# Carrying keys between chunks on VectorE, transposing the query norms, and replacing the hand-placed pieces of a one-core transformer kernel

## The chip, the cores and the metric

The kernel runs on one core of a Trainium2 chip. A core has five engines that each take their instructions in order: TensorE (PE; its weight loads are listed apart as PEld), VectorE (DVE), ScalarE (ACT), GpSimd (POOL) and SyncE (SP), which here only issues DMAs. The metric is the device time of one execution in microseconds (us), less is better.

## The reference

Everything is float32. Tokens are 2048, features 128. A block of six local-attention layers with feed-forward is applied to x, its result is added by half, a linear-attention block follows, and the six layers are applied again, also by half. Cut to what the change touches, one layer is:

```
xa  = token_shift(layer_input)                 # half of the features come one token later
q, k, v = split(xa @ Wqkv)                     # 16 heads of 64
q, k = l2norm(q) * q_scale, l2norm(k) * k_scale
q = q*cos*scale + rotate_half(q)*sin*scale     # scale grows with the token's number
k = k*cos/scale + rotate_half(k)*sin/scale
# windows of 32 queries look at their own 32 keys and the 32 before
sim  = 8 * q_window @ k_two_windows.T ; mask ; softmax ; @ v_two_windows ; @ Wo
x = xa + attention ; x = x + feed_forward(layer_norm(x))
```

A rotation by position depends only on the difference between query and key. The kernel therefore counts positions afresh in every chunk of 256 tokens, so that one table serves all chunks; the last 32 keys of a chunk, which the next chunk's first window needs, must then be turned by 256 positions into the next chunk's frame. That turn is a 2x2 mixing of the two halves of a head's features: with constants c and s per frequency, new1 = c*old1 - s*old2 and new2 = c*old2 + s*old1.

## The kernel before

**Tiling.** Activations lie transposed, features on partitions and tokens along the free axis. A layer is cut in `NAC` = 8 chunks of `AC` = 256 tokens; a chunk's attention has `STEPS` = 4 steps (two halves of 128 tokens by two groups of 8 heads). The feed-forward (`feed_forward`, L590 on) works on 512 tokens at a time, so it recurs every second chunk. There are 12 layer passes with the linear block after six.

**Order.** No scheduler decides: each function is cut in pieces by `yield`, and the table `POS` (L33 to L83) gives each piece a place (step relative to its chunk, position within the step). The pieces of all chunks are sorted by that place and emitted, which fixes each engine's queue. So in steady state the pieces of several chunks are interleaved in a pattern that repeats every four steps, and every eight steps with the feed-forward.

**One chunk, in the order of its data.**
- `project`: four groups of products (L288) give q and k in PSUM, in two feature halves. `rotate` multiplies them with the tables on VectorE (L297, "prod") and adds the two products on GpSimd (L303) into the tiles `abq` and `abk`. ScalarE squares the raw values (L309, "sq"), GpSimd adds the halves of the squares (L323), and `square_sums` sums them over features by a product on TensorE (L331, "ss").
- `norms` (L402 to L410) makes the inverse norms `rn` from `ss`: a row per head, tokens along the row. For the queries `query_norms` brings them to one row per token: two products with a selection matrix `sel[:, 2]` (L418, tile "nt"), then a copy (L424, "rq"). For the keys `spread_norms` sends them through DRAM and back as `rk`.
- `scale_keys` (called at `sk0` and `sk1` for the two groups of heads) multiplies `abk` by `rk` on VectorE (L447) and then calls `gather`, which copies keys by DMA from `abk` into `hk`, columns 32 on (L395).
- `earlier_keys` fills columns 0 to 31 of `hk`: a product of the previous chunk's last keys with the constant matrix `rot_m` (L459, tile "pk") and a ScalarE copy (L460); for a layer's first chunk a memset.
- `similarities` (L475 mask, L485 products, L497 and L498 maxima), `exponentials` (L510, with the per-row scale from `rq`), `normalised` (L520 reciprocal on VectorE, L522 multiply on GpSimd), `transposed` (L535 on TensorE, L541 copy), `values` (L562, copies L569 and L571), `output` (L578, L587).

GpSimd's queue in a step is: L522 for an earlier step, the two L323 additions, then the two L303 additions. On TensorE, L331 for a group pair stands right after L288 of the next step and ahead of L347.

Of the kernel before, what the change touches and what calls it, by code (L numbers as in the profile page):

```python
# [8 lines left out]
F32 = mybir.dt.float32  # L9
BF16 = mybir.dt.bfloat16  # L10
AF = mybir.ActivationFunctionType
ALU = mybir.AluOpType
# [3 lines left out]
P = 128  # L16
# [17 lines left out]
    "tabq": [(-11, 129), (-10, 188)],  # L34
    "tabk": [(-9, 19), (-9, 166)],
    "ss": [(-6, 25)],
    "vwin": [(0, 76)],
    "gq0": [(-6, 100)],
    "gq1": [(-4, 78)],
    "e0": [(0, 95)],  # L40
    "e1": [(0, 96)],
    "nrm": [(1, 108)],
    "qn": [(-3, 127)],
    "ek": [(-1, 91)],
    "proj": [(-9, 150), (-8, 42), (-8, 44), (-8, 45), (-8, 48), (-8, 156)],
    "vproj": [(-2, 26), (-2, 90)],
    "norms": [(-4, 47), (-4, 82), (-4, 125)],
    "rk": [(-4, 206), (-3, 27)],
    "sk0": [(-2, 94)],
    "sk1": [(-1, 176)],  # L50
    "te": [(2, 62), (2, 64)],
    "av": [(2, 149), (2, 189), (2, 190)],
    "out": [(4, 112), (4, 134)],
    "sim": [(0, 73), (0, 74), (0, 75)],
    "ff": [(11, 101), (12, 34), (12, 106), (13, 7), (13, 170), (14, 131), (15, 124), (15, 143),
        (16, 17), (16, 42), (16, 143), (16, 159), (17, 51), (17, 140), (17, 192), (18, 50),
        (18, 58), (18, 148), (18, 162), (21, 146), (21, 199)],
    "ff2": [(12, 128), (12, 194), (13, 179), (14, 65), (14, 99), (15, 52), (15, 118), (15, 147),
        (16, 20), (16, 23), (16, 122), (16, 123), (16, 130), (16, 151), (16, 152), (16, 153),
        (16, 203), (17, 5), (17, 40), (17, 97), (17, 169)],  # L60
    "ff3": [(10, 182), (10, 184), (10, 186), (10, 194), (10, 198), (10, 200), (10, 204), (11, 2),
        (11, 4), (11, 13), (11, 24), (11, 35), (11, 36), (11, 37), (11, 120), (11, 133),
        (11, 139), (11, 157), (11, 181), (11, 183), (11, 193)],
    "start0": [(-19, 114), (-17, 104), (-16, 84), (-16, 168), (-13, 41), (-10, 79)],
    "start1": [(-11, 126), (-9, 70), (-7, 31), (-7, 142), (-7, 158), (-6, 141)],
    "start2": [(-9, 19), (-7, 29), (-5, 136), (-5, 205), (-4, 11), (-4, 121)],
    "start3": [(-4, 12), (-4, 16), (-4, 46), (-4, 88), (-3, 6), (-2, 28)],
    "sums0": [(-9, 1), (-9, 49), (-8, 43), (-8, 165), (-8, 174), (-7, 43), (-7, 137), (-6, 30)],
    "sums1": [(-1, 92), (-1, 119), (0, 72), (0, 77), (1, 38), (1, 39), (2, 161), (2, 184)],
    "sums2": [(1, 185), (1, 201), (2, 167), (2, 202), (3, 63), (3, 93), (3, 160), (4, 113)],  # L70
    "sums3": [(3, 195), (4, 15), (4, 80), (4, 81), (4, 144), (4, 145), (4, 177), (4, 191)],
    "kv": [(5, 3)],
    "outs0": [(5, 9), (5, 14), (5, 109), (5, 111), (5, 173), (5, 175), (6, 54), (6, 68), (6, 71),
        (6, 138), (7, 55), (7, 61), (7, 69), (7, 135)],
    "outs1": [(6, 60), (11, 83), (11, 110), (12, 18), (13, 53), (13, 67), (13, 180), (14, 98),
        (14, 163), (15, 32), (15, 56), (15, 102), (15, 154), (17, 87)],
    "outs2": [(6, 10), (13, 21), (13, 89), (13, 164), (14, 171), (14, 178), (14, 196), (15, 33),
        (15, 116), (15, 143), (16, 66), (16, 85), (16, 132), (17, 22)],
    "outs3": [(5, 172), (15, 115), (15, 155), (16, 117), (17, 86), (17, 105), (18, 8), (18, 103),
        (18, 107), (18, 162), (18, 197), (19, 57), (19, 59), (19, 187)],  # L80
# [14 lines left out]
def kernel(ctx: ExitStack, tc: tile.TileContext, a: dict, out: bass.AP):  # L95
# [9 lines left out]
    def small(name):  # L105
        return ps_small.tile([P, CH], F32, tag="small", name=name)
# [49 lines left out]
    sq_consts = keep([P, 3, P], "sq_consts", src=a["squares"].rearrange("p a b -> p (a b)"))  # L156
    ident, hmask, rot_m = (sq_consts[:, i, :] for i in range(3))
    wqk = [load_qk(0, g) for g in range(4)]
    qks = keep([P, DEPTH, 2, 2], "qks", src=a["qks"])
    sel = keep([P, 3, 32], "sel", src=a["sel"].rearrange("p a b -> p (a b)"))  # L160
# [112 lines left out]
    def project(l, c, g):  # L273
# [3 lines left out]
        if g % 2 == 0:  # L277
            for qk, bufs in (("q", 2), ("k", 4)):
                d[qk, g // 2] = work.tile(
                    [P, 2, 2, AC], F32, tag=f"ab{qk}", name=f"ab{qk}_{nm}", bufs=bufs  # L280
                )
# [13 lines left out]
        def rotate(s):  # L295
            prod = work.tile([P, 2, 2, AC], F32, tag="prod", name=f"prod{s}_{nm}", bufs=2)
            nc.vector.tensor_tensor(  # L297
                prod,
                both[s].unsqueeze(2).to_broadcast([P, 2, 2, AC]),
                tabs[l, s].rearrange("p (u v) t -> p u v t", u=2),  # L300
                ALU.mult,
            )
            nc.gpsimd.tensor_tensor(  # L303
                d["qk"[s], g // 2][:, :, g % 2, :], prod[:, 0], prod[:, 1], ALU.add
            )
# [70 lines left out]
    def gather(l, c, qk, g2):  # L376


        d = chunk(l, c)
        off = 0 if qk == "q" else WIN  # L380
        if g2 == 0:
            d["h" + qk] = work.tile(
                [P, 8, off + AC], F32, tag=f"h{qk}", name=f"h{qk}_{d['nm']}"
            )
        for j in range(2):
            src = d[qk, g2][64 * j : 64 * j + 64]
            first = 4 * g2 + 2 * j
            if qk == "q":
                nc.sync.dma_start(
                    d["hq"][:, first : first + 2, :].rearrange("p i t -> p (i t)"),  # L390
                    src.rearrange("p u i t -> p u (i t)"),
                )
            else:
                for i in range(2):
                    nc.sync.dma_start(d["hk"][:, first + i, WIN:], src[:, :, i, :])  # L395
# [17 lines left out]
    def query_norms(l, c):  # L413

        d = chunk(l, c)
        nt = small(f"nt_{d['nm']}")
        for t in range(2):
            nc.tensor.matmul(  # L418
                nt[:, HEADS * t : HEADS * t + HEADS],
                d["rn"][:, t * P : (t + 1) * P], sel[:, 2, 0:HEADS],  # L420
                start=True, stop=True,
            )
        rq = work.tile([P, 2, HEADS], F32, tag="rq", name=f"rq_{d['nm']}", bufs=2)
        nc.vector.tensor_copy(rq.rearrange("p t h -> p (t h)"), nt[:, 0 : 2 * HEADS])  # L424
        d["rq"] = rq

# [16 lines left out]
    def scale_keys(l, c, g2):  # L443
        d = chunk(l, c)
        k = d["k", g2].rearrange("p u i t -> p u (i t)")
        r = d["rk"][:, 2 * g2 : 2 * g2 + 2, :].rearrange("p i t -> p (i t)")
        nc.vector.tensor_tensor(k, k, r.unsqueeze(1).to_broadcast([P, 2, CH]), ALU.mult)  # L447
        gather(l, c, "k", g2)

    def earlier_keys(l, c):  # L450

        d = chunk(l, c)
        first = d["hk"][:, :, 0:WIN]
        if c == 0:
            nc.gpsimd.memset(first, 0.0)
            return
        ps = small(f"pk_{d['nm']}")
        ps3 = ps[:, 0 : 8 * WIN].rearrange("p (h t) -> p h t", h=8)
        nc.tensor.matmul(ps3, rot_m, chunks[l, c - 1]["hk"][:, :, AC:], start=True, stop=True)  # L459
        nc.scalar.copy(first, ps3)  # L460

    def similarities(l, c, step):
# [31 lines left out]
        rq = d["rq"][:, t, 8 * h8 : 8 * h8 + 8].rearrange("p (i r) -> p i r", r=2)  # L494
        for par in range(2):
            yield
            nc.vector.tensor_reduce(peaks[par], sims[par], AX.X, ALU.max, negate=True)  # L497
            nc.vector.tensor_tensor(st8[:, 0, :, par], peaks[par], rq[:, :, par], ALU.mult)  # L498

    def exponentials(l, c, step, par):  # L500
# [7 lines left out]
        rq = d["rq"][:, t, 8 * h8 : 8 * h8 + 8].rearrange("p (i r) -> p i r", r=2)  # L508
        for i in range(4):
# [3 lines left out]
                scale=rq[:, i, par : par + 1],  # L513
# [75 lines left out]
    def feed_forward(layer, f):  # L589
# [52 lines left out]
        if final:  # L642
            x = work.tile([P, CH], F32, tag="gate", name=f"last_{nm}", bufs=1)
# [33 lines left out]
    def linear_sums(f):  # L677
# [14 lines left out]
        lo = work.tile([P, CH], F32, tag="gate", name=f"lo_{f}", bufs=1)  # L692
# [40 lines left out]
    def linear_out(f):  # L733
# [11 lines left out]
        z = work.tile([P, CH], F32, tag="gate", name=f"lz_{f}", bufs=1)  # L745
# [47 lines left out]
    for l in range(2 * DEPTH):  # L793
# [12 lines left out]
        for c in range(NAC):  # L806
# [15 lines left out]
            put("ek", t0, earlier_keys, l, c)  # L822
# [27 lines left out]
def _shape_constants():  # L850
# [20 lines left out]
    c, s = np.diag(back * np.cos(AC * inv)), np.diag(back * np.sin(AC * inv))  # L871
    one = np.block([[c, -s], [s, c]]).reshape(2, 32, 2, 32).transpose(1, 0, 3, 2).reshape(64, 64)
    rot_m = np.kron(np.eye(2), one)
# [11 lines left out]
        [r[:, None] == r[None, :], r[:, None] // 8 == r[None, :] // 8, rot_m], 1  # L885
    ).astype(np.float32)

    sel = np.zeros((P, 3, 32), np.float32)
    for i in range(2):
        sel[r, i, 4 * i + r // 32] = 2.0**18  # L890
    for h in range(HEADS):
        sel[32 * (h // 2 % 2) + 4 * (h // 8) + 2 * (h // 4 % 2) + h % 2, 2, h] = 1.0
    return {
        "rot": rot,
        "band": band,
# [61 lines left out]
```

## Time and profile before

| what | value |
|---|---|
| median of 3 runs | 3454.14 us (3449.54 to 3456.67) |
| the profiled execution | 3449.61 us |
| its span in the trace | 3447.8 us, so 1.8 us lie around it |
| mean granted TensorE clock | 0.982 |
| TensorE busy | 96% of the span |
| VectorE, ScalarE, GpSimd busy | 77%, 72%, 63% |
| busy share of the 16 DMA engines, queue q1 | 53.7% |

A profile row of a group names line, engine, operation, written tile <- read tiles and shapes, then the count, the busy time and the mean of one. A timeline row gives the start in us from the span's start, the length, the engine and the same names; in square brackets stands the idle time before it with what ended it. Matmul records overlap, since TensorE pipelines: what a group costs is read from its start to the next group's start. A float32 matmul shows as two records, a transpose as one. The slices of the page show that TensorE is nearly full except at the start, between the two halves of the kernel (1.6 to 1.9 ms, the linear block) and at the end.

### The profile page before, as it was taken

Reading aid. Unit: us, or ns where it says so; the run is one execution under the profiler, and the core shown is the slowest. Engines: PE = TensorE matmul, PEld = TensorE weight load, DVE = VectorE, ACT = ScalarE, POOL = GpSimd, SP = SyncE. Lnnn points to the kernel's source line nnn. Section 1 sums busy time; section 2 is a strip of 40 time slices with the busy share of each in tenths; the row PEclk is TensorE's granted clock in tenths of the full one; section 3 lists DMA queues with packets and bytes.
Section 4 is the critical chain, followed back from the end, with each engine's and each line's share of the span. In section 5 each row is a group of like instructions: output and inputs, shape, how many; then the busy total and the mean of one; then the engine's idle time right before and its main releaser. Section 6 shows DMA issues by size and latency. Waiting matters only on the chain. (4 is left out here: it accounts for less than half of the span.)

```text
span 3447.8 us, 153348 instructions
## 1 busy us (share of the span) xinstructions
PE 3293.9 (96%) x64088; PEld 2280.2 (66%) x64088; DVE 2658.6 (77%) x5068; ACT 2491.0 (72%) x8613; POOL 2182.2 (63%) x2195
## 2 busy tenths in 40 slices
PE   6999999999999999999678999999999999999998
PEld 3776776676667676676334766766767766766665
DVE  5787888878778788786446887887878888787785
ACT  4777777777777777776446777777777777777775
POOL 6766666667667667663136766666666666666661
PEclk8999999999999999999889999999999999999999
DMA  4665565556556556554004665566565565565552
GB/s 134 145 150 135 141 152 142 136 150 147 133 146 153 132 143 156 139 135 121 28 13 100 144 150 142 135 153 147 133 153 143 135 153 142 139 150 138 144 134 73
DMA packets 356445, 459.91 MB, mean 133 GB/s; under 512 B 52396, under 2 KB 218664, under 8 KB 355752
## 3 DMA queue, kind: packets, MB, share of 16 engines
q1 hardware_dynamic: 355752, 450.11, 53.7%
q8 instruction: 504, 8.26, 1.0%
q14 instruction: 189, 1.55, 0.1%
HBM read 96.53 MB, written 2.62 MB: 29 GB/s over the span
## 5 line engine op out<-in xcount | busy, mean ns | idle before, releaser
L510 ACT ACTIVATE e<-sim,st,rq 128x64 f32<-128x64 f32 x3072 | 1196.0, 410 | 352.6 <-DVE st L498 322.8
L297 DVE TENSOR_TENSOR prod<-p,tab 128x1024 f32<-128x1024 f32 x768 | 936.1, 1222 | 293.4 <-ACT sq L309 202.1
L288 PE MATMUL p<-xa,wqk 128*128 128x256 f32 x3072 | 776.5, 395 | 13.6 <-DVE xa L242 4.8
L303 POOL TENSOR_TENSOR abq<-prod 128x512 f32<-128x512 f32 x384 | 490.7, 1278 | 398.3 <-DVE prod L297 364.3
L522 POOL TENSOR_TENSOR e<-e,st 128x512 f32<-128x512 f32 x384 | 451.8, 1177 | 425.5 <-DVE st L520 242.8
L309 ACT ACTIVATE sq<-p 128x512 f32<-128x512 f32 x768 | 438.8, 603 | 350.5 <-PE ss L331 159.2
L303 POOL TENSOR_TENSOR abk<-prod 128x512 f32<-128x512 f32 x384 | 492.4, 1282 | 242.6 <-DVE prod L297 217.8
L510 ACT ACTIVATION_READ_ACCUMULATOR e<-sim,st,rq 128x1 f32 x3072 | 643.3, 209 | 0.0
L288 PEld LDWEIGHTS p<-xa,wqk 128*128 128x128 f32 x3072 | 557.7, 191 | 105.8 <-issue 9.8
L323 POOL TENSOR_TENSOR sq<-sq 128x256 f32<-128x256 f32 x768 | 580.1, 776 | 0.2
L562 PEld LDWEIGHTS av<-eT,vw 64*64 64x64 f32 x18432 | 392.3, 135 | 227.8 <-ACT hk L460 59.6
L562 PE MATMUL av<-eT,vw 64*64 64x32 f32 x18432 | 434.9, 221 | 2.9 <-DVE eT L541 1.8
L347 PE MATMUL pv<-wv,xa 128*128 128x512 f32 x768 | 417.5, 626 | 7.8 <-DVE oT L571 7.8
L578 PE MATMUL y<-oT,wo 128*128 128x128 f32 x3072 | 390.5, 280 | 0.2 <-DVE oT L571 0.2
L578 PEld LDWEIGHTS y<-oT,wo 128*128 128x128 f32 x3072 | 362.5, 192 | 36.1 <-issue 22.6
L562 PE MATMUL av<-eT,v 64*64 64x32 f32 x6144 | 384.3, 219 | 0.0
L535 PEld LDWEIGHTS te<-sq_consts,e 128*128 128x128 f32 x1536 | 188.5, 141 | 236.1 <-issue 166.9
L497 DVE TENSOR_REDUCE sim<-sim 128x4 f32<-128x256 f32 x768 | 325.9, 424 | 21.6 <-PE sim L485 20.7
L485 PE MATMUL sim<-hk,hq 64*32 64x64 f32 x24576 | 333.3, 223 | 0.1
L562 PEld LDWEIGHTS av<-eT,v 64*64 64x64 f32 x6144 | 318.8, 135 | 0.0
L612 PE MATMUL pf<-xc,w 128*128 128x512 f32 (+1 forms) x576 | 304.6, 615 | 11.5 <-POOL xc L600 9.3
L485 PEld LDWEIGHTS sim<-hk,hq 64*32 64x32 f32 x24576 | 306.0, 105 | 0.3
(140 smaller groups left out, 4270.9 us busy)
## 6 DMA issues: line engine op xcount, KB each, us to landing
hq<-abq SPq DMA_DIRECT2D x384, 256.0 KB
hk<-abk SPq DMA_DIRECT2D x768, 128.0 KB
vw<-v SPq DMA_DIRECT2D x768, 128.0 KB
rk<-rkd SPq DMA_DIRECT2D x384, 128.0 KB
vw<-v SPq DMA_DIRECT2D x744, 64.0 KB
wqk<-in_Wqk SPq DMA_DIRECT2D x48, 256.0 KB
tab<-in_rot SPq DMA_DIRECT2D x24, 512.0 KB
wv<-in_Wv SPq DMA_DIRECT2D x24, 256.0 KB
```

The costliest lines, as they stand in the source:

```text
L288: nc.tensor.matmul(both[s][:, u, :], wqk[g][:, 2 * s + u, :], xs, start=True, stop=True)
L297: nc.vector.tensor_tensor(prod, both[s].unsqueeze(2).to_broadcast([P, 2, 2, AC]), tabs[l, s].rearrange("p (u v) t -> p u v t", u=2), ALU.mult,
L303: nc.gpsimd.tensor_tensor(d["qk"[s], g // 2][:, :, g % 2, :], prod[:, 0], prod[:, 1], ALU.add)
L309: nc.scalar.activation(sq, both[s], AF.Square)
L323: nc.gpsimd.tensor_tensor(sq[:, 0, :], sq[:, 0, :], sq[:, 1, :], ALU.add)
L347: nc.tensor.matmul(ps, xa[:, ti * P : (ti + 1) * P], wv[j], start=True, stop=True)
L485: nc.tensor.matmul(sims[par][WIN * b : WIN * b + WIN, i, :], d["hq"][rows, 4 * h8 + i, at : at + WIN], d["hk"][rows, 4 * h8 + i, at : at + ...
L497: nc.vector.tensor_reduce(peaks[par], sims[par], AX.X, ALU.max, negate=True)
L510: nc.scalar.activation(e[:, i, par, :], d["sims", step][par][:, i, :], AF.Exp, bias=st8[:, 0, i, par : par + 1], scale=rq[:, i, par : par ...
L522: nc.gpsimd.tensor_tensor(ef, ef, st8[:, 1].rearrange("p i r -> p (i r)").unsqueeze(2).to_broadcast([P, 8, SK]), ALU.mult,)
L562: nc.tensor.matmul(av[u][r : r + 64, m, WIN * b : WIN * b + WIN], d["vs", t][u][b][:, at : at + DH], d["eT", step][64 * u : 64 * u + 64, i ...
L578: nc.tensor.matmul(y[:, 0:P], wo[:, i, :], d["oT", t].rearrange("p h u m q -> p (h u m) q")[:, i, :], start=(i == 0), stop=(i == 7),)
```

## The change

1. **Keys of the chunk before.** `abk` gets 32 more columns per head group in front. After scaling a chunk's keys, VectorE writes the turned last 32 keys into the front of the *next* chunk's `abk`, with per-partition constants `turn` (c, s, -s): one tensor_scalar over 128 columns and two scalar_tensor_tensor over 64 columns. `gather` then copies 288 columns instead of 256, and `earlier_keys` with its product, its PSUM tile and its ScalarE copy is gone. In a layer's last chunk there is no turn; in its first the memset moves to `abk`, once for each group.
2. **Query norms.** The two products with `sel[:, 2]` become two transposes of `rn` by `ident`; the copy picks 32 of the transposed columns; `step_norms` gives the later readers their heads in the new order.
3. **Memory.** `rot_m` and `sel[:, 2]` go, `turn` (128x3) comes. The tile `gate` (512 columns) goes, and its users at the ends of the two halves and in the linear block take a half of a `prod` tile.
4. **Places.** `POS` is new throughout. Compared by the built instruction order, TensorE, ScalarE and VectorE keep their order within the repeating pattern, apart from what items 1 and 2 remove and add: VectorE has the three turn instructions directly behind each L447. SP issues one weight load earlier by one or two places in three spots of a layer. In the linear block the fourth tile's pieces (`outs3`) come later than before, behind the first tile's, and a few pieces near the kernel's start change places.

```diff
     def scale_keys(l, c, g2):
         d = chunk(l, c)
-        k = d["k", g2].rearrange("p u i t -> p u (i t)")
-        r = d["rk"][:, 2 * g2 : 2 * g2 + 2, :].rearrange("p i t -> p (i t)")
-        nc.vector.tensor_tensor(k, k, r.unsqueeze(1).to_broadcast([P, 2, CH]), ALU.mult)
+        k = d["k", g2]
+        r = d["rk"][:, 2 * g2 : 2 * g2 + 2, :].unsqueeze(1).to_broadcast([P, 2, 2, AC])
+        nc.vector.tensor_tensor(k[..., WIN:], k[..., WIN:], r, ALU.mult)
+        if c == 0:
+            nc.gpsimd.memset(k[..., 0:WIN], 0.0)
         gather(l, c, "k", g2)
-
-    def earlier_keys(l, c):
-
-        d = chunk(l, c)
-        first = d["hk"][:, :, 0:WIN]
-        if c == 0:
-            nc.gpsimd.memset(first, 0.0)
-            return
-        ps = small(f"pk_{d['nm']}")
-        ps3 = ps[:, 0 : 8 * WIN].rearrange("p (h t) -> p h t", h=8)
-        nc.tensor.matmul(ps3, rot_m, chunks[l, c - 1]["hk"][:, :, AC:], start=True, stop=True)
-        nc.scalar.copy(first, ps3)
+        if c + 1 < NAC:
+
+            last, first = k[..., AC:], chunk(l, c + 1)["k", g2][..., 0:WIN]
+            nc.vector.tensor_scalar(first, last, turn[:, 0:1], None, ALU.mult)
+            for u in range(2):
+                nc.vector.scalar_tensor_tensor(
+                    first[:, u], last[:, 1 - u], turn[:, u + 1 : u + 2], first[:, u],
+                    ALU.mult, ALU.add,
+                )
```

```diff
     def query_norms(l, c):
-        nt = small(f"nt_{d['nm']}")
+        nt = small(f"nt_{d['nm']}").rearrange("p (t r) -> p t r", t=4)
         for t in range(2):
-            nc.tensor.matmul(
-                nt[:, HEADS * t : HEADS * t + HEADS],
-                d["rn"][:, t * P : (t + 1) * P], sel[:, 2, 0:HEADS],
-                start=True, stop=True,
-            )
-        rq = work.tile([P, 2, HEADS], F32, tag="rq", name=f"rq_{d['nm']}", bufs=2)
-        nc.vector.tensor_copy(rq.rearrange("p t h -> p (t h)"), nt[:, 0 : 2 * HEADS])
+            nc.tensor.transpose(nt[:, t, :], d["rn"][:, t * P : (t + 1) * P], ident)
+        rq = work.tile([P, 2, 2, 8], F32, tag="rq", name=f"rq_{d['nm']}", bufs=2)
+        nc.vector.tensor_copy(rq, nt[:, 0:2, 0:64].rearrange("p t (i r) -> p t i r", r=32)[..., 0:8])
         d["rq"] = rq
+
+    def step_norms(d, t, h8):
+
+        return d["rq"][:, t, :, 4 * h8 : 4 * h8 + 4].rearrange("p i (j r) -> p j i r", r=2)
...
-            put("ek", t0, earlier_keys, l, c)
```

## The prediction

> **What bounds the kernel now.** First the page: TensorE's busy share and its row of slices, then VectorE's row.
>
> ```profile
> PE 3293.9 (96%) x64088; PEld 2280.2 (66%) x64088; DVE 2658.6 (77%) x5068; ACT 2491.0 (72%) x8613; POOL 2182.2 (63%) x2195
> ...
> PE   6999999999999999999678999999999999999998
> ...
> DVE  5787888878778788786446887887878888787785
> ```
>
> TensorE is full outside the start, the middle and the end, so at first sight whatever leaves its queue is won. But a busy share can hold waits, so next comes the timeline of TensorE over one four-step pattern (columns: start, length, group).
>
> ```profile
> 1009.09 0.60 PE L535 MATMUL te<-sq_consts,e 128*128 128x128 f32 x4
> 1009.62 0.30 PE L475 MATMUL sim<-band,ident_b 64*32 64x256 bf16 x8
> ...
> 1010.51 0.70 PE L459 MATMUL pk<-hk,sq_consts 128*128 128x256 f32 x2
> 1011.05 1.02 PE L210 MATMUL mean<-xf,mean_w 128*128 128x512 f32 x2
> ...
> 1014.99 1.20 PE L331 MATMUL ss<-sq,sel 128*32 128x256 f32 x8
> 1016.12 1.13 PE L347 MATMUL pv<-wv,xa 128*128 128x512 f32 x2
> ...
> 1026.52 0.62 PE L418 MATMUL nt<-sel,rn 128*128 128x16 f32 x4
> 1026.99 2.82 PE L637 MATMUL yf<-h,w 128*128 128x512 f32 x6
> ```
>
> Start to start, "pk" costs 0.54 us, "nt" 0.47, four transposes 0.53 (0.13 each). And "ss" takes 1.13 here; at 1032.73 the same eight records take 0.57. So 0.56 us is a wait inside a queue that looks full. It recurs in every second chunk (1082.31, 1148.11 and 1213.92 also take 1.13). The wait view names the squares that GpSimd adds (L323). What are these late for? VectorE and GpSimd in the same stretch:
>
> ```profile
> 1001.57 1.22 DVE L297 TENSOR_TENSOR prod<-p,tab 128x1024 f32<-128x1024 f32 x1 [2.94 <-ACT sq L309]
> ...
> 1005.16 1.22 DVE L447 TENSOR_TENSOR abk<-abk,rk 128x1024 f32<-128x1024 f32 x1
> 1006.30 0.19 DVE L520 RECIPROCAL st<-st 128x8 f32<-128x8 f32 x1
> ...
> 1011.94 0.19 DVE L520 RECIPROCAL st<-st 128x8 f32<-128x8 f32 x1
> 1012.05 1.18 DVE L447 TENSOR_TENSOR abk<-abk,rk 128x1024 f32<-128x1024 f32 x1
> ```
>
> ```profile
> 1012.28 1.85 POOL L522 TENSOR_TENSOR e<-e,st 128x512 f32<-128x512 f32 x1 [0.48 <-DVE st L520]
> 1014.09 1.41 POOL L323 TENSOR_TENSOR sq<-sq 128x256 f32<-128x256 f32 x2
> ```
>
> From 1001.57 VectorE has no gap until 1015.5. Its second reciprocal (1011.94) releases GpSimd's L522, L323 follows in GpSimd's queue and ends at 1015.50, and "ss" ends 0.6 later. Backward, the product at 1001.57 waited for ScalarE's square, and ScalarE is busy without a gap from 991.35, where it waited for TensorE's L288. So from 991 to 1015.5 a chain ScalarE, VectorE, GpSimd runs *beside* TensorE and ends 0.56 later than it. Both "nt" (993.60) and "pk" of this chunk lie beside that chain.
>
> The other kind of chunk (even numbers, with L618 ahead of the second L447) is near the same edge:
>
> ```profile
> 1177.73 1.04 POOL L522 TENSOR_TENSOR e<-e,st 128x512 f32<-128x512 f32 x1 [0.21 <-DVE st L520]
> 1178.74 2.39 POOL L323 TENSOR_TENSOR sq<-sq 128x256 f32<-128x256 f32 x2
> ```
>
> L323 ends at 1181.13, "ss" starts at 1181.30: 0.17 us of slack. Of four such chunks in a layer two are like this, one waits 0.4 (1115.06) and one 1.3 (1048.17).
>
> **Part 1, products removed.** TensorE loses 84 "pk" of 0.54 us: 45 us. "nt" becomes two transposes, by the row of "te" 2 x 0.13 = 0.27 for 0.47: 0.20 x 96 = 19 us. Were TensorE the bound everywhere: 3449.6 - 64 = 3386. ScalarE loses 84 copies of 0.37; its exponentials there wait for VectorE's L498 anyway, so nothing.
>
> **Part 2, the turn.** Each of 168 L447 gets three VectorE instructions behind it. No row has just these. The nearest for the tensor_scalar has its very size, SBUF to SBUF:
>
> ```profile
> L730 DVE TENSOR_SCALAR wl_kv<-sq_consts,wl_ksum x1: 286/286/286, 1719.6 to 1719.6; 128x128 f32<-128x128 f32 x1
> ```
>
> [...] For 64 columns of scalar_tensor_tensor: L662 takes 425 ns at 256, L727 292 at 128, so 225 at 64; L409 (371 at 256) gives 170. I take 0.20. A dependent instruction starts 0.04 after its forerunner (1010.87 + 0.42 to 1011.33), an independent one 0.08 before its end (1006.30). The next instruction moves by 0.04 + 0.29 + 0.04 + 0.20 + 0.12 = **0.69 us** (bounds 0.5 and 0.8). That is 116 us more of VectorE, to some 80% of the span, and it isn't spread: at the first L447 of a chunk it stands ahead of the L520 that releases GpSimd, in a stretch without a gap.
>
> *Odd chunks* (1, 3, 5; 7 has no turn): L323 ends at least 0.69 later; TensorE comes 0.74 earlier and waits the more. Absolutely +0.69.
> *Even chunks* (0, 2, 4, 6): GpSimd's own queue from L522 (1171.63) to 1177.52 carries part; L522 moves by 0.5 to 0.7, less 0.17 slack.
>
> [...] L447 reads two tensors in SBUF. Its row of before:
>
> ```profile
> L447 DVE TENSOR_TENSOR abk<-abk,rk x192: 1172/1225/4678, 56.6 to 3383.1; 128x1024 f32<-128x1024 f32 x192
> ```
>
> At 1012.28 L522, 1.04 us elsewhere, takes 1.85 while L447 runs; at 1045.04 an L447 takes 4.63 and ends 1.08 after a GpSimd run that lasted to 1048.6. [...] I take 0.2 for L323, and keep 0 and the long wait for the range.
>
> **Edits costed at nothing, with their cover.** The extra wait of the turn on the copy that last read its target is for a copy one chunk (35 us) old. The key copies are issued behind L447, not behind the turn, and are an eighth larger on queues at 54%. The weight loads that SP issues earlier (0.4 to 0.7 us each) delay `rk`, issued by 1031.5 and needed at 1037.0. The extra memsets are 12 of some 0.2 us (estimate from L455's 0.3) on GpSimd. Half a `prod` tile for `gate`: a rotation may wait for it at two layer ends and in the linear block, 0 to 4 us in all. In the linear block the fourth tile's step leaves the place ahead of the first tile's layer norm; its four VectorE instructions of 0.7 us were in the way there, 3 us gained, and 6 lost or gained are the bounds.
>
> **Sum.** Odd chunks with a turn: 0.69 + 0.2 = 0.9, three in a layer: 2.7. Even chunks: two with slack 0.7 each (0.69 + 0.2 - 0.17), one without 0.9, and the one at 1048.17 1.4, since there TensorE also waited (1050.06) for VectorE's L571 *behind* the second L447, so both turns count: 3.7. The gain of "nt" in four even chunks lies outside the chain: -0.8. Per layer 5.6, twelve layers 67. At the two starts of the layers no feed-forward fills VectorE for some eight chunks; the removed products are gained there instead: -6. Linear block: -3. 3449.6 + 58 = **3508 us**, against a median of 3454 in the runs shown (the profiled execution is 4.5 below it): 1.6 to 1.7% slower.
>
> **Rivals.**
> 1. *TensorE is the bound after all: faster.* For it: 96% busy, and "ss" waits in half the chunks only. Against: the steady 0.56 us, and the 0.17 of slack. It needs the 0.69 us to vanish on VectorE: slack of 0.7 in front of L520. VectorE's idle before 1001.57 (2.9 us) isn't such slack, since it ends with ScalarE's square. With half to all of the 64 us: 3386 to 3420. It decides if the turn delays L323 by less than about 0.1 us per chunk.
> 2. [...] If each second turn waits for GpSimd's run to end, VectorE is 1.4 to 2 us later; its 0.75 us of idle at 1016.27 takes part, and some 0.8 us reach TensorE in 84 chunks: 67 us more, 3575. For it: ten L447 of over 4.5 us. [...]
> [...]
> 4. *It doesn't do what it says:* the instruction order shows the products gone and three instructions behind each L447; no chance given.
>
> **How the numbers follow.** The forecast 0.65 (its own range 3478 to 3540), rival 1 0.18, rival 2 0.09, rival 3 0.08. The range leaves out the lower part of rival 1 and most of rival 2: 3412 to 3550. No change is within 0.2% (7 us), about what a measurement of this kernel can tell. Faster takes rival 1 and a little of rival 3: 0.19; no change 0.05; slower 0.76.
>
> **What would show it.** Right: "ss" (L331) at some 2 us instead of 1.13 in odd chunks and 1.5 to 2 instead of 0.57 in even ones, with L323 named; TensorE's busy share down to 93 or 94%; the three turn instructions together near 0.7 us at the first L447 of a chunk and longer at the second; L522 or L323 lengthened there. Wrong: "ss" still at 0.57 to 1.2, or the turn in a gap of VectorE. If the span falls by 45 to 64 us, the chain wasn't the bound, and step "VectorE has no gap ahead of L520" failed. If L323 moved as said but TensorE gained elsewhere, the sum over chunks failed, not its step.

## The result, and the profile after

| | median of runs, us | profiled execution: span, us | granted clock |
|---|---|---|---|
| before | 3454.22 (3449.54 to 3456.67, 4 runs) | 3447.8 | 0.982 |
| after | 3511.96 (3505.87 to 3515.56, 4 runs) | 3513.7 | 0.981 |

The ratio is 1.0167, with a 95% interval of 1.0148 to 1.0186: 1.7% slower. The profiled execution of after is the longest of its runs (3515.56 us) and that of before one of the shortest, so the spans differ by 65.9 us and the medians by 58. First the page of after: engines (busy us, share of the span, instructions) and two rows of slices.

```profile
PE 3275.3 (93%) x63728; PEld 2222.5 (63%) x63728; DVE 2849.6 (81%) x5572; ACT 2468.5 (70%) x8529; POOL 2181.4 (62%) x2207
...
PE   6999999999999999998778999999999999999998
...
DVE  6888888888888888886537888888888888888885
```

TensorE has 360 matmuls less and is busy for 93% instead of 96%. VectorE got 191 us more, to 81%, and now shows an 8 in nearly every slice: most of its slices of 7 are filled. GpSimd's sum is as it was (2182.2 before). Next TensorE's waits, of after and of before (what waited, for what, us, times, longest):

```profile
PE ss L332 <- POOL sq L324: 71.3, 99, 4.8
PE p L289 <- ACT v L352: 33.8, 42, 1.4
...
PE p L289 <- DVE xf L588: 10.2, 32, 0.4
```

```profile
PE ss L331 <- POOL sq L323: 25.7, 15, 3.5
PE te L535 <- ACT oT L569: 20.0, 33, 1.1
```

The wait at "ss" has grown as forecast. Two waits were next to nothing before (4.2 and 0.2 us): "p" for ScalarE's copy of v, and "p" for VectorE's L588. The wait of "te" for ScalarE is gone from the list. (Lines of after: L446 is the key scaling, L453 and L455 the turn, L521 the reciprocal, L523 GpSimd's product, L324 its squares, L332 "ss", L588 the addition of the output.)

Now the turn itself, in the timeline of VectorE of after, at the first key scaling of an odd chunk and at its second:

```profile
1027.22 1.23 DVE L446 TENSOR_TENSOR abk<-abk,rk 128x1024 f32<-128x1024 f32 x1
1028.48 0.29 DVE L453 TENSOR_SCALAR abk<-abk,turn 128x128 f32<-128x128 f32 x1
1028.81 0.48 DVE L455 SCALAR_TENSOR_TENSOR abk<-abk,turn,abk 128x64 f32<-128x64 f32 x2
1029.20 0.20 DVE L521 RECIPROCAL st<-st 128x8 f32<-128x8 f32 x1
1029.32 0.54 DVE L588 TENSOR_TENSOR xf<-y,xa 64x128 f32<-64x128 f32 x2
...
1034.92 1.17 DVE L446 TENSOR_TENSOR abk<-abk,rk 128x1024 f32<-128x1024 f32 x1
1036.13 0.95 DVE L453 TENSOR_SCALAR abk<-abk,turn 128x128 f32<-128x128 f32 x1
1037.11 1.32 DVE L455 SCALAR_TENSOR_TENSOR abk<-abk,turn,abk 128x64 f32<-128x64 f32 x2
```

From the start of L446 to that of the reciprocal it is 1.98 us, against 1.14 before (1005.16 to 1006.30): the first turn costs 0.84. The second lasts from 1036.13 to 1038.43, 2.3 us, and GpSimd is at work beside it (over all second turns of after it is 1.5 us in most even chunks, 2.3 in most odd ones, 1.9 on average):

```profile
1035.15 1.85 POOL L523 TENSOR_TENSOR e<-e,st 128x512 f32<-128x512 f32 x1 [0.47 <-DVE st L521]
1036.96 1.40 POOL L324 TENSOR_TENSOR sq<-sq 128x256 f32<-128x256 f32 x2
```

These two GpSimd rows are as long as before (1.85 and 1.41). What reaches TensorE, in the same chunk (the last column names the wait):

```profile
1028.52 1.13 PE L289 MATMUL p<-xa,wqk 128*128 128x256 f32 x4
1030.00 1.10 PE L289 MATMUL p<-xa,wqk 128*128 128x256 f32 x4 [0.35 <-DVE xf L588]
1030.94 1.02 PE L348 MATMUL pv<-wv,xa 128*128 128x512 f32 x2
...
1037.26 0.62 PE L332 MATMUL ss<-sq,sel 128*32 128x256 f32 x2
1038.41 0.63 PE L332 MATMUL ss<-sq,sel 128*32 128x256 f32 x6 [0.53 <-POOL sq L324]
1038.97 1.13 PE L348 MATMUL pv<-wv,xa 128*128 128x512 f32 x2
```

The same "p" and "pv" before:

```profile
1006.40 1.99 PE L288 MATMUL p<-xa,wqk 128*128 128x256 f32 x8
1008.23 1.02 PE L347 MATMUL pv<-wv,xa 128*128 128x512 f32 x2
```

Eight "p" and the step to "pv" took 1.83 us; here 2.42. "ss" takes 1.71 instead of 1.13, start to start. A third wait of an odd chunk stands two steps later: "nt" starts 0.31 later, since it waits for ScalarE's squares. Together 0.59 + 0.58 + 0.31, less the 0.54 of "pk", which is gone, come to 0.94 us, which is what such a chunk loses.

One stretch of an odd chunk will be used below: from the "p" of the step ahead of "ss" (1028.52) to the "pv" behind "ss" (1038.97). It takes 10.45 us here and took 9.72 before (1006.40 to 1016.12); the medians of 44 such chunks are 10.38 and 9.72.

Where along the kernel the time is lost can be read from one instruction that each chunk has, "nt": its start in after less its start in before, in us, at the first chunk of each layer (layers are counted from 0; layer 0 starts at 0.0). The last row is for experiment e1 below, which leaves the turn out.

| layer | 1 | 2 | 3 | 4 | 5 | 6 | 6, behind the linear block | 7 | 8 | 9 | 10 | 11 | end |
|---|---|---|---|---|---|---|---|---|---|---|---|---|---|
| after | 9.4 | 13.1 | 19.0 | 24.8 | 30.1 | 38.9 | 30.9 | 36.4 | 42.5 | 48.2 | 53.9 | 58.7 | 65.9 |
| e1 | -0.4 | -2.3 | -3.1 | -3.7 | -4.9 | -5.8 | -13.5 | -14.3 | -14.7 | -16.6 | -18.3 | -19.6 | -19.1 |

Layers 2 to 4 and 7 to 10 lose 4.8 to 6.1 us each, layer 1 only 3.7. The first layer (0) loses 9.4, the last layers of the two halves (5 and 11) 8.8 and 7.2, and the linear block gives back 8.0. Within a steady layer an odd chunk with a turn loses 0.8 to 1.2, three of the even ones 0.2 to 0.6 each and the fourth 1.0 to 1.4.

### The profile page after: what moved, and what is told of

Read it like the earlier page. It is cut to its first block, busy times and chain, and to the rows that moved or that the text cites. A ratio compares the mean times of both kernels' runs of the same rounds, so it can differ in the third digit from the quotient of the medians.

```text
span 3513.7 us, 153374 instructions
## 1 busy us (share of the span) xinstructions
PE 3275.3 (93%) x63728; PEld 2222.5 (63%) x63728; DVE 2849.6 (81%) x5572; ACT 2468.5 (70%) x8529; POOL 2181.4 (62%) x2207
## 5 line engine op out<-in xcount | busy, mean ns | idle before, releaser
L289 PE MATMUL p<-xa,wqk 128*128 128x256 f32 x3072 | 792.9, 398 | 50.1 <-ACT v L352 33.8
L523 POOL TENSOR_TENSOR e<-e,st 128x512 f32<-128x512 f32 x384 | 451.3, 1175 | 476.6 <-DVE st L521 377.7
L310 ACT ACTIVATE sq<-p 128x512 f32<-128x512 f32 x768 | 446.0, 602 | 404.9 <-DVE prod L298 184.5
L324 POOL TENSOR_TENSOR sq<-sq 128x256 f32<-128x256 f32 x768 | 577.2, 772 | 0.0
```

Source lines behind the costliest of these rows:

```text
L289: nc.tensor.matmul(both[s][:, u, :], wqk[g][:, 2 * s + u, :], xs, start=True, stop=True)
L310: nc.scalar.activation(sq, both[s], AF.Square)
L324: nc.gpsimd.tensor_tensor(sq[:, 0, :], sq[:, 0, :], sq[:, 1, :], ALU.add)
L523: nc.gpsimd.tensor_tensor(ef, ef, st8[:, 1].rearrange("p i r -> p (i r)").unsqueeze(2).to_broadcast([P, 8, SK]), ALU.mult,)
```

## The experiments

Each time is a median; "before" is the kernel before beside it on the same chip, and the ratio is to that.

| run | what it is | us | before, us | ratio, 95% interval |
|---|---|---|---|---|
| e1 | after, one memset for each turn | 3429.62 | 3451.09 | 0.9935 (0.9918 to 0.9952) |
| e2 | after, v copied earlier | 3510.58 | 3451.09 | 1.0170 (1.0155 to 1.0186) |
| e3 | after, turns moved | 3555.60 | 3451.09 | 1.0302 (1.0286 to 1.0317) |
| e4 | before, "nt" transposed | 3444.53 | 3451.09 | 0.9983 (0.9968 to 0.9998) |
| e5 | after, six memsets for each turn | 3535.26 | 3448.22 | 1.0251 (1.0234 to 1.0268) |
| e6 | after, first turn only | 3491.96 | 3448.22 | 1.0121 (1.0106 to 1.0136) |
| e7 | after, second turn only | 3454.70 | 3448.22 | 1.0018 (1.0010 to 1.0025) |
| e8 | after, odd sk0 early | 3501.37 | 3448.22 | 1.0149 (1.0134 to 1.0165) |
| e9 | after, squares first | 3488.28 | 3451.97 | 1.0102 (1.0087 to 1.0117) |
| e10 | before, squares first | 3428.64 | 3451.97 | 0.9934 (0.9918 to 0.9950) |
| e11 | e9 and e8 together | 3468.58 | 3451.97 | 1.0044 (1.0028 to 1.0061) |
| e12 | before with e4, e10, odd sk0 early | 3432.23 | 3448.46 | 0.9951 (0.9937 to 0.9964) |

**e1: no turn.**

```diff
-            nc.vector.tensor_scalar(first, last, turn[:, 0:1], None, ALU.mult)
-            for u in range(2):
-                nc.vector.scalar_tensor_tensor(
...
+            nc.vector.memset(chunk(l, c + 1)["k", g2][..., 0:WIN], 0.0)
```

> The changed kernel with the three instructions of each turn replaced by one VectorE memset of the same columns (the earlier keys of a chunk are zero, the turn is left out). Chain theory (the turn stands ahead of the reciprocal that releases GpSimd, and at the second key scaling beside GpSimd): most of the 67 us that the sum gave to the turn go, 3440 to 3460 us. Bank theory (half of the loss is TensorE waiting at p for ScalarE's copy of v, because p1 took the PSUM bank of pv; 34 us in the trace): the turn is worth only some 30, 3475 to 3490, and the wait at p stays at 30 to 40 us. TensorE as the only bound without the turn: 3390 to 3420.

3429.6 us: the turn was 82 us (80 by the ratios), more than any theory gave it. The larger key copies and the new places are in e1 too, so they are no part of these 82. What is left is 21 us better than before, though TensorE has lost 64 us of products. (e1's own memsets may hide some of the gain: one moves the reciprocal by 0.14 us, so 84 of them are 12 us at most, an estimate.) Where the rest of the products went shows in one odd chunk of e1, on TensorE:

```profile
1002.66 1.99 PE L289 MATMUL p<-xa,wqk 128*128 128x256 f32 x8
...
1010.81 0.62 PE L332 MATMUL ss<-sq,sel 128*32 128x256 f32 x2
1011.80 0.63 PE L332 MATMUL ss<-sq,sel 128*32 128x256 f32 x6 [0.37 <-POOL sq L324]
1012.37 1.12 PE L348 MATMUL pv<-wv,xa 128*128 128x512 f32 x2
```

From the first "p" to the last "pv" it is 9.71 us. Before, with "pk" of 0.54 us between, it was 9.72, and the medians of 44 such chunks are the same two numbers. "ss" starts earlier and waits longer: the stretch is as long as a path beside it, which begins at this "p" and runs over ScalarE's square, VectorE's second rotation, its copy eT, the maxima, the reciprocal, GpSimd's product and the squares (its start is read off e8 below). The wait of "p" for v stayed, at 32.6 us.

**e2: the new wait at "p".** The tiles in PSUM named "small" share five banks (`bufs=5` of `ps_small`), and which tile gets whose bank is settled when the kernel is built. In chunks 0, 2, 4 and 6 of most layers the third p1 takes the bank of "pv" in after (42 times in all, the count of the new wait); before, only chunk 2 did (10 times), and the others had that of "av". ScalarE's copy of v stands behind the gelu, so it is late.

```diff
-    "vproj": [(-2, 23), (-2, 85)],
+    "vproj": [(-2, 23), (-2, 45)],
```

> The changed kernel with ScalarE's copy of v placed behind the squares instead of behind the gelu, so that p1 no longer takes a bank that this copy still reads; the turn stays. Chain theory: the wait at p (34 us) goes, but GpSimd's squares come no earlier, so TensorE waits the more at ss: 3500 to 3512 us, with the ss wait up by 20 to 30. Bank theory: the 34 us go for good, 3475 to 3485, and the ss wait stays near 71 us.

3510.6 us, as the chain theory had it: the 33.8 us at "p" vanish from the list, and 31.1 us of "te" waiting for ScalarE's oT take their place ("ss" stays at 66.7). The disappearance of a wait of 1% of the span changed the time by 1.4 us, less than the runs scatter. The theory was wrong in the wait that takes its place: it had named "ss".

**e3: the turn elsewhere.** Places only; the turn became pieces of its own, with the same three instructions.

```diff
+    "tk0": [(-2, 103.5)],
+    "tk1": [(1, 45.5)],
```

> The changed kernel with the same turn, but the first one of a chunk behind the reciprocal instead of ahead of it, and the second one 10 us later between the two rotations of the next step. Chain theory: ss waits as before the change, the removed products partly gained: 3440 to 3465 us, with ss waits at 20 to 40 us. Load theory (VectorE simply has 116 us more to do and has no gap, wherever it stands): 3500 to 3515. Bank theory: the wait at p stays at some 34 us, so not below 3450.

3555.6 us, 44 worse than after, where 50 to 70 better had been expected. VectorE and GpSimd of e3 at a first turn (L524 is the reciprocal, L526 GpSimd's product, L591 the addition of the output):

```profile
1039.89 0.20 DVE L524 RECIPROCAL st<-st 128x8 f32<-128x8 f32 x1
1040.01 0.29 DVE L456 TENSOR_SCALAR abk<-abk,turn 128x128 f32<-128x128 f32 x1
1040.33 1.73 DVE L458 SCALAR_TENSOR_TENSOR abk<-abk,turn,abk 128x64 f32<-128x64 f32 x2
1041.98 0.58 DVE L591 TENSOR_TENSOR xf<-y,xa 64x128 f32<-64x128 f32 x2
```

```profile
1040.25 1.04 POOL L526 TENSOR_TENSOR e<-e,st 128x512 f32<-128x512 f32 x1 [2.50 <-DVE st L524]
```

Behind the reciprocal GpSimd is at work, since the reciprocal is what starts it. The two L458, 0.48 together ahead of it, take 1.73, and L591 comes 2.1 us after the reciprocal instead of 0.1. Of the 336 scalar_tensor_tensor of e3, 205 began while GpSimd worked and took 1.05 us on average; in after 146 did, with 0.64. "p" then waits 41.7 us for L591. All three ranges missed.

**e4: the transposes alone.** The function query_norms and the readers of its result, as in the diff of the change, in the kernel before.

> The kernel before with the transposed query norms alone. Chain theory: 0.2 us gained in the four even chunks of a layer and at the two starts, nothing in odd chunks: 3440 to 3446 us. TensorE as the only bound: 96 times 0.2 = 19 us, 3433 to 3437.

3444.5 us (eight runs from 3437 to 3460), 6.6 better than before beside it and in the chain theory's range, where TensorE as the only bound would give 19. Here too 36.1 us at "p" for v appear (42 times), with "pk" still in place: the transposes alone shift the banks.

**e5: length without operands.**

```diff
+            for _ in range(6):
+                nc.vector.memset(chunk(l, c + 1)["k", g2][..., 0:WIN], 0.0)
```

> Each turn of the changed kernel replaced by six VectorE memsets of the same columns (the turn is left out, earlier keys are zero). A memset took 165 ns in e1 whether GpSimd ran or not, and one of them moved the next instruction by 0.14 us, so six put 0.84 us on VectorE like an undisturbed turn, but read no operand. Path theory (the prediction: the time of the turn on VectorE is the loss): 3490 to 3510 us. Port theory (the turn's waits for GpSimd, 81 us in the records of after, are at least half of it): 3450 to 3470.

The six were to stand for an undisturbed turn, but in its trace they follow each other by 0.26 us, so they last 1.46 us, not 0.84. At 3535 us, 106 above e1 and above both ranges, they say one thing: time on VectorE at these two places is dear even if it touches no operand. That a turn made longer by GpSimd isn't needed for the loss is shown; the equal-length comparison failed.

**e6 and e7: half a turn.**

```diff
+            if g2 == 0:
...
+            else:
+                nc.vector.memset(chunk(l, c + 1)["k", g2][..., 0:WIN], 0.0)
```

(e7 has the branches the other way round.)

> The turn only behind the first key scaling of a chunk, one memset in its place behind the second (half of the turn is left out). Path theory: the first turn stands ahead of the reciprocal and is most of the 82 us: 3480 to 3495 us. Port theory: the first turn runs while GpSimd is idle and costs the smaller part: 3445 to 3465.

> The turn only behind the second key scaling, one memset behind the first (half of the turn is left out). Path theory: behind the reciprocal it costs little, 3440 to 3455 us. Port theory: it waits for GpSimd there and holds the rotation behind it: 3470 to 3490.

Over e1 the first turn costs 62 us and the second 25 (64 and 29 by the ratios to before, since e1 ran on another chip), with 82 for both. Per turn that is 0.74 us for the first, which is 0.70 longer than the memset in its place: it comes out at the end almost one to one. The second occupies VectorE for 1.9 us on average and costs 0.30. The odd chunks say the same: from "p" to "pv" the median is 10.47 us in e6 and 9.71 in e7. Place, not length, makes the price; path theory holds, and port theory with its 40 us or more for the second falls. e6 lies inside the path theory's range; e7 is at its upper edge.

**e8: less in front of the reciprocal.** In odd chunks the first key scaling and its turn go to where VectorE stands idle.

```diff
+    "sk0e": [(-2, 45.5)],
...
+                early = "e" if g2 == 0 and c % 2 else ""
+                put("sk" + "01"[g2] + early, t0, scale_keys, l, c, g2)
```

> The changed kernel, whole, with the first key scaling of every odd chunk and its turn moved ahead of the second rotation of its step, where VectorE stands idle for 3.0 to 3.9 us in every odd chunk. Path theory: 1.2 + 0.84 us leave the stretch that ends at ss in four odd chunks of a layer, which is more than the 0.6 to 1.2 us that TensorE waits there; the even chunks stay as they are: 3455 to 3480 us. If the turn's place doesn't matter, or GpSimd's product beside it holds it as in e3: 3505 to 3530.

3501.4 us: both rows of expectations missed it. In one odd chunk the reciprocal comes 3.47 us after the second rotation (1018.89 to 1022.36) instead of 5.55 (1023.65 to 1029.20), so the 2 us are won on VectorE, and "p" no longer waits for the addition of the output. But from "p" to "pv" it is again 9.71 us (1023.83 to 1033.54, also the median): in steady layers each odd chunk with a turn wins only some 0.7 against after, and then the path of e1 ends it. VectorE of e8 in that chunk shows where the path begins:

```profile
1025.07 1.23 DVE L299 TENSOR_TENSOR prod<-p,tab 128x1024 f32<-128x1024 f32 x1 [0.65 <-PE p L290]
1026.56 1.22 DVE L299 TENSOR_TENSOR prod<-p,tab 128x1024 f32<-128x1024 f32 x1 [0.27 <-ACT sq L311]
1027.71 0.68 DVE L543 COPY eT<-te 128x512 f32<-128x512 f32 x1
```

VectorE is idle ahead of both rotations: the first waits for this step's "p", the second for ScalarE's square of it. From there to the reciprocal it has no gap, so the path doesn't begin as far back as 991, but at the "p" of its own step. In e1 the second rotation starts at the same distance from "p", 2.73 us, and before too, where VectorE came free at that very moment. In after it starts 3.50 us behind "p": VectorE has no gap there from the rotation at 1023.65 to the end of the second turn.

**e9, e10: cut that path.** GpSimd adds the squares ahead of its product, so "ss" needs no reciprocal. The edit of e9 (in e10 the last place goes from 156 to 105):

```diff
-    "proj": [(-9, 154), (-8, 41), (-8, 43), (-8, 44), (-8, 47), (-8, 158)],
+    "proj": [(-9, 154), (-8, 41), (-8, 43), (-8, 44), (-8, 47), (-8, 100)],
```

> The changed kernel, whole, with GpSimd's two additions of squares (L324) placed ahead of its product with the reciprocals (L523) in each step instead of behind it, so that ss no longer waits for the reciprocal. Path theory (the loss reaches TensorE through reciprocal, L523, L324, ss): the ss wait falls from 71 us to under 25 us and the time to 3430 to 3465 us. Rival (VectorE's own lateness reaches TensorE just as well at te, av and p): the waits only change their names, 3490 to 3515 us.

> The kernel before with the same exchange on GpSimd. Path theory: the steady 0.56 us at ss in odd chunks go and half of the rest, 20 to 35 us: 3415 to 3435 us. Rival: within 5 us of before. If it beats e9, the changed kernel loses even without the path through the squares.

Both gain 23 to 24 us, and e10 is the fastest kernel here, 0.7% below before. Its "ss" waits 15.8 us. The changed kernel is still 60 us above it. The waits of e9:

```profile
PE p L289 <- ACT v L352: 42.5, 42, 1.4
PE pv L348 <- DVE oT L572: 26.9, 34, 1.0
PE av L563 <- DVE eT L542: 25.5, 54, 1.1
PE p L289 <- DVE xf L588: 17.0, 32, 0.6
PE ss L332 <- POOL sq L324: 15.2, 6, 4.7
```

"ss" is down as foreseen, from 71.3 to 15.2, but three other waits for VectorE grew, and the time, 3488.3, lies far above the path theory's range and 2 us below the rival's. So the rival was right for the turn: its 0.8 us reaches TensorE by several ways, and with "ss" shut the others carry it. The waits show these ways; how much goes by each isn't known.

**e11, e12: put together.** e11 is e9 with the edit of e8. e12 is the kernel before with the edits of e4 and e10 and the early first key scaling.

> e9 with the first key scaling and its turn in odd chunks moved into VectorE's idle time as in e8. Path theory: VectorE has 2 us less ahead of the reciprocal in odd chunks, which now only helps te and av: 5 to 25 us below e9. Rival: no gain over e9, as e8 gained only 11 us over the changed kernel.

> The kernel before, whole, with its products for the earlier keys kept, and three edits: the transposed query norms (e4), GpSimd's squares ahead of its product (e10), and the first key scaling of odd chunks in VectorE's idle time (as in e8, there is no turn behind it). If the gains add: 3452 less 23 (e10), 7 (e4) and 10 to 20 (e8 and e11) is 3402 to 3412 us. If TensorE is the bound by now, the key scaling's place is worth nothing: 3420 to 3430.

e11 gains 20 us over e9, within its range, more than e8 gained: with the path through the squares cut, VectorE's time does count. e12 gains 16 us, not more than e10's 23, and is 2 us above the higher of its two ranges: the gains don't add. It has the wait of "p" for v again (35.0 us, 42 times), from the transposes.

## Why the prediction came out right, step by step

Forecast 3508, with a range of 3478 to 3540; measured 3512. The main step, the first turn at its full length on a path that TensorE waits for, is shown (e1, e6); the closeness of the total is in part luck.

- **TensorE isn't the bound: right, and shown.** With the products gone and no turn (e1) 21 us were won, not 64. The sum had 19 us for this (0.8 a layer, the starts and the linear block). That these two agree is in part luck: 7.7 of e1's 19.1 in the trace come in the linear block, where 3 were forecast, and next to nothing at the starts, where 6 were.
- **Length of the first turn: 0.69 forecast, 0.84 measured.** The missed term is the scalar_tensor_tensor: 0.20 estimated, 0.28 measured (270 ns at least in 336 rows). The estimate drew a line through rows of other operands, which doesn't hold for these.
- **"Absolutely" one to one: right.** 54 us of the sum were for first turns (0.69 in each odd chunk with a turn; 0.52, 0.52, 0.69 and 0.69 in the even ones); e6 gave 62 to 64.
- **The way it takes: half right.** "From 991 to 1015.5 a chain" was too long. Without a turn in the way, what ends an odd chunk starts at the "p" of its own step (e1, e8); VectorE's stretch without a gap from 1001.57 ends level with that path, so the turn could lengthen it at once. And L520, L522, L323, "ss" is one way of several: in odd chunks as much enters at "p" (0.59) as at "ss" (0.58). That "p" waits for L588, queued behind the turn and the reciprocal, to free the bank of y. The prediction named what stands behind the turn only up to the reciprocal.
- **GpSimd beside the second turn: sum right, term wrong.** 23 us were in the sum for second turns, 25 to 29 measured (e7). But no run shows the 0.2 that it has for a longer L323: all L323 and L324 took 596.0 us before and 592.8 after, all L522 and L523 451.8 and 451.3. What the runs show in its place is VectorE's turn made longer while GpSimd was at work: an L453 that began with GpSimd idle took 0.29 us (85), one beside it 0.80 (83); an L455 took 0.28 (190) and 0.64 (146). Added up over all turns of after, VectorE loses some 93 us to this, against turns of 0.81 us (the 81 us in the expectation of e5 were too few), and its busy time grew by 191 us instead of 116. The long wait that rival 2 feared came, 1.5 us in most odd chunks and 0.7 in most even ones, but most of it was swallowed by slack behind the second key scaling. (Before, 37 L447 took between 1.38 and 2.0 us and ten above 4.5; all 47 began while GpSimd was at work.)
- **The tensor_scalar's 0.29.** It was taken from one row (L730, 286 ns), and it is what an L453 took that began with GpSimd idle (0.29, 85 times). One such row can't say what comes beside GpSimd: L453, with a single tensor input, took 0.80 on average there, while a memset of the same size took 165 ns in all of 168 cases of e1, 80 of them beside GpSimd:

```profile
L452 DVE MEMSET abk<- x168: 165/165/165, 61.0 to 3337.1; 128x128 f32 x168
```

  What in L453 makes the difference is not shown: it reads a tensor and a constant, the memset neither, and no run separates the two. All three instructions of the turn took longer beside GpSimd, not only the two L455.
- **Layers: right in the steady ones.** 5.6 us each were forecast, 4.8 to 6.1 measured in layers 2 to 4 and 7 to 10; layers 1, 5 and 11, at 3.7, 8.8 and 7.2, were not seen apart. Odd chunks 1.0 for 0.9. "ss" took 1.7 us in odd chunks, where some 2 were named, and 1.5 in even ones (medians), the lower end of the range; part of the delay shows at "p".
- **Starts and linear block: wrong, and they cancel in part.** "The removed products are gained there instead: -6" failed. The first layer lost 9.4 us where 2.6 was forecast, and layer 6, where it is fed by no feed-forward either, lost 5.5. Without the turn (e1) these layers gain 0.4 and 0.8: the turn costs there as well, and the removed products bring next to nothing. The linear block gave 8.0, not 3, and e1 shows the same 7.7 without the turn, so it belongs to the other edits. Which of them isn't known: none was tried by itself there.

The total is thus nearer to the result than its parts: a first turn too cheap and starts too hopeful against a linear block too poor.

## What to carry to other kernels

An engine at 96% can still be the follower: measure the same stretch with and without the removed work (here 9.72 and 9.71 us) before counting it as won. When work moves to an engine that stands ahead of a releasing instruction, price it by its place: 0.84 us ahead of the reciprocal cost 0.74 each, 1.9 us behind it 0.30. But a place behind isn't free by itself: list everything behind the insertion (L588 freed a bank) and what the release starts beside it (e3), and expect a wait that is taken away to come back under another name (e2, e9).

## What the runs showed of the hardware

- A tensor_scalar of 128 columns with one tensor input (L453 of after) took 0.29 us where it began with GpSimd idle (85 times) and 0.80 on average, up to 1.32, where GpSimd was at work (83 times). A memset of the same columns took 165 ns in all 168 cases of e1, 80 of them beside GpSimd.
- In the odd chunk above, the one that began later took longer: GpSimd's L523, started 0.23 us after VectorE's L446, took 1.85 us, against 1.04 in the step before (1029.57), and the turn, begun at 1036.13 while L523 ran (to 1037.00), took 2.3 us, against the 0.84 of the first.
- A change of two small products alone (e4) altered which PSUM bank "p" gets, and the waits with it: "te" for ScalarE's oT fell from 20.0 to 0.5 us, "p" for its copy of v rose from 4.2 to 36.1. That is settled in the built program, not on the chip, but in the trace it looks like any other wait.
